# Regrouping the PSUM banks of a transformer-block kernel: score buffers, dense sums and the transposed maxima

## The chip, the cores and the metric

The kernel runs on one core of a Trainium2 chip. The metric is the device time of one launch in microseconds (us). It is the median of three runs for the kernel before, and a profiled execution of its own stands beside it.

A core has five engines that run side by side, each through its own list of instructions in order: TensorE (PE) multiplies matrices, VectorE (DVE) and ScalarE (ACT) work element by element and can read PSUM, GpSimd (POOL) works on SBUF, and SyncE (SP) issues DMAs. TensorE writes its results to PSUM, which has eight banks of 128 partitions x 512 fp32 values. A bank can be written again only when the engines that read it are done.

## The reference

One transformer block for 16 batches of 512 tokens and 512 channels, in fp32: attention with 32 heads of 16 channels, rotated by position, causal, and then a gated feed-forward layer of 1408 inner channels with weights of -1, 0 and 1. Cut to what matters:

```
x  = inputs                                     # 16 x 512 x 512
n  = layernorm(x)
q, k, v = n @ Wq.T + bq, n @ Wk.T + bk, n @ Wv.T + bv
q, k = rope(q), rope(k)                         # by head, two rotations
p  = softmax(causal(q @ k.T / 4))               # 32 heads, 512 x 512
x  = x + layernorm((p @ v) @ Wo.T + bo)
n  = layernorm(x)
g, u = (n @ gate_w.T) * gate_s, (n @ up_w.T) * up_s
x  = x + layernorm((silu(g) * u) @ down_w.T * down_s)
```

## The kernel before

**Periods, groups, steps.** `front` prepares batch 0 and part of batch 1. Then `batches` runs one period for each batch `b`. In a period the attention of batch `b` is computed in 8 groups of 4 heads, each in `STEPS = 6` steps (`one_step(work, n, i)`, group `n`, step `i`). The dense products of the neighbouring batches are laid between the steps: `run_list` takes a list of single matmuls, each with a cost, and lets a share of it follow the scores of each step. For `b = 0` the list is `first_list`, which holds little: the rest of v, then q and k of batch 1, the transposes of batch 2's normalised input, and `fold_bias`. It is spread over 56 steps, ten of which come ahead of the first group (`n = -2` and `-1`), so that a step carries about one dense matmul. From `b = 1` on the list holds a whole batch's products, and a step carries four to ten dense matmul records. This document calls the steps of `b = 0` the first period.

**A step.** `scores(n, m, i)` emits two kinds of scores, each for two heads, with their matmuls interleaved head by head:

- `st`, the scores of group `n` with keys on the partitions, minus the row maxima (`mx`), which the last of each three matmuls adds. ScalarE makes the softmax weights of them (`weights`: an exponential `pt<-st`), and GpSimd then zeroes what lies beyond the diagonal. `i // 2` is the third of the keys' triangle: 512 columns, 128 + 384 columns, 256 columns. `i % 2` is the pair of heads.
- `s`, the scores of a coming group `m` with queries on the partitions. VectorE takes their negative row maxima (`maxima`, instructions `s<-s,mask` with a readout `nm`).

At step 2 `turn_maxima` transposes the maxima of group `n + 1` on TensorE (`pm`), ScalarE and VectorE split them into two parts (`nmh`, `nml`), and DMAs put these into `mx`. Then the step's share of dense matmuls comes. At step 3 and at step 0 of the next group `values` multiplies weights and values (`av`), 8 records at step 3 and 24 at step 0, and at the end ScalarE copies the sum out (`ot`).

**Dense sums.** `product` takes a bank with `psum` at its first matmul and calls a `tail` after its last. For q and k (`qk_block`, products `pq` and `pk`) the tail is two ScalarE instructions `ys` and one VectorE instruction `ya`, both reading the bank. Some items later follow `ya<-ya,ys` (VectorE), `yh` (ScalarE) and `yl` (GpSimd). For the transposes of a normalised block (`turn`, `px`, four transposes into one bank) the tail is a ScalarE copy, in the first period `ht<-px`. For `pv` it is a copy to `v`; for `fold_bias` (`po`) a VectorE addition.

**The eight banks.** `ps_s` holds two tiles `s` of one bank; `ps_t` one tile `st` of two banks; `ps_av` one bank `av`; `ps_d` three banks in turn, for all that `psum` hands out: the dense sums and `pm`. Ahead of the first group (`n < 0`) the steps with odd `i` put their `s` scores into the `st` tile.

The names in the profile are those of the tiles; line 49 is a helper that records every operation, so the names, not the lines, tell what an instruction is.

Of the kernel before, what the change touches and what calls it, by code (L numbers as in the profile page):

```python
# [10 lines left out]
FP = mybir.dt.float32  # L11
FR = mybir.dt.float32r
AF = mybir.ActivationFunctionType
# [5 lines left out]
P = 128  # L19
T = 512  # L20
# [18 lines left out]
class InOrder:  # L39


    def __init__(self, tc, engine):
        self.tc, self.engine = tc, engine
# [10 lines left out]
class Block:  # L54
# [15 lines left out]
    def __init__(self, tc, ctx, a):  # L70
        self.tc, self.a = tc, a
        nc = self.nc = tc.nc
        self.pe = InOrder(tc, nc.tensor)
        self.dve = InOrder(tc, nc.vector)
        self.act = InOrder(tc, nc.scalar)
        self.pool = InOrder(tc, nc.gpsimd)
        self.sp = InOrder(tc, nc.sync)
        self.B = a["x"].shape[0]
        self.F = a["wd"].shape[0]
        self.NF = self.F // P  # L80
        pool = lambda name, **k: ctx.enter_context(tc.tile_pool(name=name, **k))
        self.const = pool("const", bufs=1)
        self.work = pool("work", bufs=2)
        self.small = pool("small", bufs=5)
        self.dram = pool("dram", bufs=1, space=bass.MemoryType.DRAM)
        self.ps_s = pool("ps_s", bufs=2, space=bass.MemoryType.PSUM)
        self.ps_t = pool("ps_t", bufs=1, space=bass.MemoryType.PSUM)
        self.ps_av = pool("ps_av", bufs=1, space=bass.MemoryType.PSUM)
        self.ps_d = pool("ps_d", bufs=3, space=bass.MemoryType.PSUM)
        self.todo = defaultdict(list)  # L90
        self.step = 0
        self.exact = False

        self.spare = [(self.B - 2, 2), (self.B - 2, 3), (self.B - 1, 3)]
        for name in "xts xns xnts x1s x2ts ks qs mxs nms pts avs ots ocs rcs wts hts wfs yas xrs pieces".split():
            setattr(self, name, {})
        self.constants()
# [3 lines left out]
        return (pool or self.work).tile(shape, dtype, tag=tag, name=tag, **kw)  # L101

    def psum(self, name):
        return self.ps_d.tile([P, 512], FP, tag="d", name=name)

    def later(self, steps, f, *args):
        self.todo[self.step + steps].append((f, args))
# [454 lines left out]
    def scores(self, n, m, i):  # L562

        third, pair = divmod(i, 2)
        ps = pm = None
        todo = []
        if 0 <= n < self.B * NG:
            ps = self.ps_t.tile([P, 2, T], FP, tag="st", name="st")
            q, ks, mx = self.qs[n], self.ks[n], self.mxs[n]
            for j in range(2):  # L570
                h = 32 * (2 * pair + j)
                r, r2 = slice(h, h + 32), slice(h, h + 2)
                todo.append([])
                for kb, at, w in ST_SETS[third]:
                    out, x = ps[:, j, at : at + w], q[r, T - w : T]
                    todo[-1] += [
                        (out, ks[0][r, ts(kb, P)], x, True, False),
                        (out, ks[1][r, ts(kb, P)], x, False, False),
                        (out, self.one[r2, :], mx[r2, T - w : T], False, True),
                    ]  # L580
        if 0 <= m < self.B * NG:
            if n < 0 and i % 2:
                both = self.ps_t.tile([P, 2, T], FP, tag="st", name="st")
                pm = [both[:, j, :] for j in range(2)]
            else:
                pm = [self.ps_s.tile([P, T], FP, tag="s", name="s") for _ in range(2)]
            q, ks = self.qs[m], self.ks[m]
            for j in range(2):
                h = 32 * (2 * (1 - pair) + j)
                r = slice(h, h + 32)  # L590
                todo.append([])
                for qb, at, w in S_SETS[third]:
                    out, x = pm[j][:, at : at + w], q[r, ts(qb, P)]
                    todo[-1] += [(out, x, ks[0][r, 0:w], True, False), (out, x, ks[1][r, 0:w], False, True)]

        for k in range(max((len(t) for t in todo), default=0)):
            for t in todo:
                if k < len(t):
                    out, l, r, first, last = t[k]
                    self.pe.matmul(out, l, r, start=first, stop=last)  # L600
        if ps is not None:
            self.weights(n, third, pair, ps)
        if pm is not None:
            for j in range(2):
                self.maxima(m, third, 2 * (1 - pair) + j, pm[j])
# [9 lines left out]
            )  # L615

    def turn_maxima(self, m):
        p = self.psum("pm")
        self.pe.transpose(p[0:16, 0:P], self.nms.pop(m).rearrange("p j b -> p (j b)"), self.ident)
        hi, lo = [self.tile([16, P], i, bufs=1, dtype=FR) for i in ("nmh", "nml")]  # L620
        self.act.copy(hi, p[0:16, 0:P])
        self.dve.tensor_tensor(lo, p[0:16, 0:P], hi, ALU.subtract)
        mx = self.mxs[m] = self.tile([P, T], "mx", bufs=2, dtype=FR)

        def put():
            for i, t in enumerate((hi, lo)):
                self.sp.dma_start(out=mx[i:P:32, :].bitcast(FP), in_=t.bitcast(FP))

        self.later(1, put)

    def weights(self, n, third, pair, ps):
        w = sum(w for _, _, w in ST_SETS[third])
        if third < 2 or pair == 0:
            pt = self.tile([P, 2, T], "pt", bufs=4)
            self.pts[n, third, pair] = pt
        if third == 2:
            if pair:
                pt = self.pts[n, 2, 1] = self.pts[n, 2, 0]
            pt = pt[:, pair, :].rearrange("p (j t) -> p j t", j=2)
        self.act.activation(pt[:, :, :w], ps[:, :, :w], AF.Exp, scale=0.25)  # L640
        if third == 1:
            d = pt[:, :, 0 : 2 * P]
            pat = [[0, 2], [0, 2], [1, P]]
        else:
            d = pt[:, :, 0:P]
            pat = [[0, 2], [1, P]]
        self.pool.affine_select(out=d, in_=d, compare_op=ALU.is_ge, fill=0.0, base=0, pattern=pat, channel_multiplier=-1)
# [303 lines left out]
    def batches(self):  # L951
        B = self.B
        work = self.run_list(self.first_list(), 56)
        self.load_group(0)
        for n, i0 in ((-2, 2), (-1, 0)):
            for i in range(i0, STEPS):
                self.one_step(work, n, i)
        for b in range(B):
            if b:
                if b < B - 1:  # L960
                    L = self.dense(b)
                    L += self.gate_ups(b - 1, b + 2 if b + 2 < B else None, b + 2 == B)
                    if b < B - 2:
                        L += self.downs(b - 1, b + 2)
                else:
                    down = [self.downs(b - 2, None, tbs, True, True) for tbs in ((0, 1), (2, 3))]
                    L = down[0] + self.dense(b, down[1]) + self.gate_ups(b - 1, None, True)
                work = self.run_list(L, NG * STEPS)
            for g in range(NG):
                for i in range(STEPS):  # L970
                    self.one_step(work, b * NG + g, i)
        L = [(0, lambda half=half: self.load_w(B - 1, "o", half)) for half in range(2)]
        work = self.run_list(L + self.downs(B - 2, None, (0, 1), True, True), STEPS + 2)
        for i in range(STEPS + 2):
            self.one_step(work, B * NG + i // STEPS, i % STEPS)
        for _, f in self.laid(self.last_list()):
            f()
# [61 lines left out]
```

## Time and profile before

| | |
|---|---|
| median of 3 runs | 3222.02 us (3218.17 to 3222.62) |
| profiled execution | 3215.86 us, of which the span 3214.0 us |
| busy share of the span | PE 96%, DVE 59%, ACT 48%, POOL 43% |
| 108 to 260 us, the first period's groups | PE busy 128.34 of 152.00 us, mean clock 0.85 |
| 260 to 3054 us, the later periods | PE busy 2752.18 of 2794.00 us, mean clock 1.00 |
| exponential `pt<-st`, 128x1024 and 128x512 | 1.024 us and 0.596 us |

How to read it: the page divides the span into 40 slices of 80 us and gives each engine's busy share in tenths; `PEclk` is the clock granted to TensorE in tenths of full speed. "Waits" list who waited for whom: total us, how often, the longest. In the timeline a line is start, duration, engine, operation, out<-in with the shape, and in brackets the idle time just before it and what ended it. `PEld` is the load of a matmul's stationary operand, which can run beside a matmul. An fp32 matmul of the dense products appears as two records, so that "x2" there is one matmul. Durations come from one execution, so a sum made of them is measured against 3215.86 us.

### The profile page before, as it was taken

How to read it: one execution, taken by the hardware profiler on the slowest of the kernel's cores; microseconds unless marked ns; L12 is line 12 of the kernel's file. 1: busy time of each engine (PE TensorE's matmuls, PEld its weight loads, DVE VectorE, ACT ScalarE, POOL GpSimd, SP SyncE). 2: the span in 40 equal slices, each digit the busy share in tenths (PEclk: the TensorE clock that was granted, in tenths of full speed). 3: DMA queues.
4: the chain of work that ended last, by engine and by line, in shares of the span. 5: the costliest groups of instructions: out<-in, count | busy, mean ns of one | idle time of the engine just before them, and what ended most of it. 6: DMA issues, size and time to landing. Idle time of an engine off the chain costs nothing.

```text
span 3214.0 us, 59287 instructions
## 1 busy us (share of the span) xinstructions
PE 3097.9 (96%) x21258; PEld 1743.3 (54%) x21258; DVE 1888.0 (59%) x5911; ACT 1542.7 (48%) x2243; POOL 1383.9 (43%) x1933
## 2 busy tenths in 40 slices
PE   6889999999999999999999999999999999999988
PEld 2334555646556464655646455464655646455556
DVE  5465656556565665656566565665656566565633
ACT  5354545454554544545454554544455454453432
POOL 4143445443544534345443544534345453443343
PEclk9899999999999999999999999999999999999999
DMA  6454534445353443525345352543535345343422
GB/s 251 166 166 152 189 101 163 139 149 172 108 190 106 160 164 123 195 93 177 127 152 173 127 185 96 168 147 123 195 101 183 122 147 172 123 156 105 131 97 71
DMA packets 227441, 471.41 MB, mean 147 GB/s; under 512 B 40976, under 2 KB 45072, under 8 KB 226704
## 3 DMA queue, kind: packets, MB, share of 16 engines
q1 hardware_dynamic: 226704, 466.47, 43.1%
q8 instruction: 170, 2.79, 0.4%
q10 hardware_dynamic: 432, 1.05, 0.1%
q14 instruction: 135, 1.11, 0.1%
HBM read 345.79 MB, written 125.30 MB: 147 GB/s over the span
## 4 chain that ended last, share of the span: by engine, by line
PE 83%; DVE 2%; DMA 2%; ACT 2%; POOL 1%; issue 1%; SPq 0%; ACTq 0%; DVEq 0%; POOLq 0%
PE st L49 16%; PE pu L49 11%; PE pg L49 10%; PE av L49 9%; PE pd L49 9%; PE po L49 7%; PE pq L49 6%; PE pv L49 5%; PE pk L49 5%; PE s L49 3%; DMA kl<-kd 2%; PE px L49 1%; ACT pt L49 1%; DVE s L49 1%; PE pm L49 1%
## 5 line engine op out<-in xcount | busy, mean ns | idle before, releaser
L49 DVE CUSTOM_DVE_ANT_0 s<-s,mask 128x512 f32<-128x512 f32 (+1 forms) x2034 | 974.9, 510 | 713.8 <-PE s L49 530.8
L49 ACT ACTIVATE pt<-st 128x1024 f32<-128x1024 f32 (+1 forms) x768 | 677.0, 882 | 755.9 <-PE st L49 746.9
L49 POOL TENSOR_SCALAR_AFFINE_SELECT pt<-pt 128x256 f32<-128x256 f32 (+1 forms) x768 | 393.8, 513 | 1202.3 <-ACT pt L49 1200.0
L49 PEld LDWEIGHTS st<-q,kh 32*128 32x128 f32 x2048 | 191.3, 183 | 463.3 <-issue 225.6
L49 PE MATMUL st<-q,kh 32*128 32x512 f32 (+3 forms) x2048 | 411.2, 398 | 22.3 <-ACT pt L49 20.9
L49 PE MATMUL s<-kh,q 32*128 32x512 f32 (+1 forms) x2034 | 411.6, 399 | 17.2 <-DVE nm L49 8.8
L49 PE MATMUL s<-kl,q 32*128 32x512 f32 (+1 forms) x2034 | 340.7, 321 | 11.2 <-DMA kl<-kd 11.2
L49 PE MATMUL av<-pt,v 128*32 128x512 f32 (+3 forms) x4096 | 336.0, 447 | 0.0
L49 PE MATMUL st<-q,kl 32*128 32x512 f32 (+3 forms) x2048 | 333.5, 322 | 0.0
L49 PE MATMUL st<-mx,one 2*128 2x512 f32 (+3 forms) x2048 | 333.0, 321 | 0.0
L49 POOL TENSOR_TENSOR hl<-ht,hh 128x512 fp32r<-128x512 f32 (+1 forms) x192 | 229.6, 1196 | 184.3 <-ACT hh L49 176.7
L49 PE MATMUL pd<-wd,hl 128*128 128x512 f32 x704 | 288.9, 410 | 9.2 <-POOL hl L49 9.2
L49 PE MATMUL pd<-wd,hh 128*128 128x512 f32 x704 | 290.9, 413 | 2.2 <-ACT hh L49 2.2
L49 DVE DVE_READ_ACCUMULATOR2_ANT nm<- 128x1 f32 x2048 | 288.8, 141 | 0.0
L49 PE MATMUL pg<-xntf,wf 128*128 128x512 f32 x704 | 287.4, 408 | 1.5 <-ACT xntf L49 1.5
L49 PE MATMUL pu<-xntfl,wf 128*128 128x512 f32 x704 | 284.3, 404 | 0.0
L49 PE MATMUL pu<-xntf,wf 128*128 128x512 f32 x704 | 283.9, 403 | 0.0
L49 PE MATMUL pg<-xntfl,wf 128*128 128x512 f32 x704 | 281.5, 400 | 0.6 <-DVE xntfl L49 0.6
L49 PE MATMUL po<-w,oc 128*128 128x512 f32 x512 | 244.6, 610 | 3.7 <-DMA w<-in_wo 3.7
L49 PE MATMUL pq<-xnta,w 128*128 128x512 f32 x480 | 237.6, 626 | 6.9 <-ACT xntf L49 6.3
L49 PE MATMUL pk<-xnta,w 128*128 128x512 f32 x480 | 238.3, 615 | 4.3 <-DVE ya L49 3.7
L49 POOL TENSOR_TENSOR yl<-ya,yh 128x512 fp32r<-128x512 f32 x128 | 163.3, 1276 | 169.4 <-ACT yh L49 169.4
(118 smaller groups left out, 5021.8 us busy)
## 6 DMA issues: line engine op xcount, KB each, us to landing
wf<-wgs SPq DMA_DIRECT2D x176, 512.0 KB
q<-qd SPq DMA_DIRECT2D x128, 256.0 KB
kh<-kd SPq DMA_DIRECT2D x128, 256.0 KB
kl<-kd SPq DMA_DIRECT2D x128, 256.0 KB
od<-ot SPq DMA_DIRECT2D x128, 256.0 KB
w<-in_wo SPq DMA_DIRECT2D x34, 512.0 KB
xr<-in_x SPq DMA_DIRECT2D x66, 256.0 KB
w<-in_wq SPq DMA_DIRECT2D x32, 512.0 KB
```

The costliest lines, as they stand in the source:

```text
L49: return self.tc.keep_in_program_order(f(*args, **kwargs))
```

## The change

In the first period (and in the ten steps ahead of it) only one of the three banks of `ps_d` serves the dense sums. The other two become a second place for `st`, used in the steps with odd `i`, while even steps use `ps_t` as before; ahead of the first group they take the odd steps' `s` scores. As two one-bank tiles take the place of one two-bank tile there, the exponential of an odd step is two instructions, one for each head, instead of one. From the second period on the three banks serve the dense sums in turn again and every step uses `ps_t`. In all periods `pm` is put into the bank of `av` and no longer takes a turn among the three.

```diff
-        self.ps_d = pool("ps_d", bufs=3, space=bass.MemoryType.PSUM)
+        self.ps_d = pool("ps_d", bufs=1, space=bass.MemoryType.PSUM)
+        self.banks, self.bank = 3, 0
...
     def psum(self, name):
-        return self.ps_d.tile([P, 512], FP, tag="d", name=name)
+        self.bank = (self.bank + 1) % self.banks
+        return self.ps_d.tile([P, 512], FP, tag=f"d{self.bank}", name=name)
+
+    def two_banks(self, other, name):
+        if other and self.banks == 1:
+            return [self.ps_d.tile([P, T], FP, tag=f"d{1 + j}", name=name) for j in range(2)]
+        return self.ps_t.tile([P, 2, T], FP, tag="st", name=name)
...
     def scores(self, n, m, i):
...
-            ps = self.ps_t.tile([P, 2, T], FP, tag="st", name="st")
+            ps = self.two_banks(i % 2, "st")
...
             if n < 0 and i % 2:
-                both = self.ps_t.tile([P, 2, T], FP, tag="st", name="st")
-                pm = [both[:, j, :] for j in range(2)]
+                pm = self.two_banks(True, "s")
...
     def turn_maxima(self, m):
-        p = self.psum("pm")
+        p = self.ps_av.tile([P, T], FP, tag="av", name="pm")
...
     def weights(self, n, third, pair, ps):
...
-        self.act.activation(pt[:, :, :w], ps[:, :, :w], AF.Exp, scale=0.25)
+        if isinstance(ps, list):
+            for j in range(2):
+                self.act.activation(pt[:, j, :w], ps[j][:, :w], AF.Exp, scale=0.25)
+        else:
+            self.act.activation(pt[:, :, :w], ps[:, :, :w], AF.Exp, scale=0.25)
...
     def batches(self):
...
+        self.banks = 1
         for n, i0 in ((-2, 2), (-1, 0)):
...
             if b:
+                self.banks = 3
```

More of the change, by code (lines that the diff above doesn't have):

```diff
@@ L574, in scores @@
                 for kb, at, w in ST_SETS[third]:
-                    out, x = ps[:, j, at : at + w], q[r, T - w : T]
+                    out, x = (ps[j] if isinstance(ps, list) else ps[:, j])[:, at : at + w], q[r, T - w : T]
                     todo[-1] += [
```

## The prediction

> **What bounds the kernel now.** I read the page first: TensorE is busy for 3097.9 of 3214.0 us, and its slices say where it is not.
>
> ```profile
> PE   6889999999999999999999999999999999999988
> PEclk9899999999999999999999999999999999999999
> ```
>
> Only the first three slices and the tail are below 9. Then busy time by stage: from 260 to 3054 us PE has 2752.18 of 2794.00 us at clock 1.00, so dense matmuls bound it there. In the first period's 48 steps, 108 to 260 us, it has 128.34 of 152.00 us at a clock of 0.85. That is the room: 23.7 us idle and 0.15 x 152 = 23 us of withheld clock. Third, the waits of 120 to 260 us:
>
> ```profile
> PEld st L49 <- ACT pt L49: 32.9, 32, 2.3
> PE st L49 <- ACT pt L49: 13.0, 14, 2.0
> PE s L49 <- DVE nm L49: 4.9, 13, 0.7
> ```
>
> A weight load can wait beside a running matmul, so the price of one score buffer `st` looks like the second line, 13.0 us in 14 waits. The timeline tells whether it is. Such a wait:
>
> ```profile
> 180.48 0.60 ACT L49 ACTIVATE pt<-st 128x512 f32<-128x512 f32 x1 [0.74 <-PE st L49]
> ...
> 180.66 0.47 DVE L49 CUSTOM_DVE_ANT_0 s<-s,mask 128x256 f32<-128x256 f32 x1
> ...
> 181.13 0.38 PE L49 MATMUL st<-q,kh 32*128 32x256 f32 x2 [0.75 <-ACT pt L49]
> ```
>
> PE resumes when the exponential ends. But the same step's `s` matmuls, next in PE's queue, need the maxima of the last step to be read, and that VectorE instruction ends at 180.66 + 0.47 = 181.13 too. The other pair of banks is free no earlier.
>
> Fourth, the end of a dense sum, the place where one bank must do for three:
>
> ```profile
> 181.69 1.13 PE L49 MATMUL pk<-xnta,w 128*128 128x512 f32 x2
> ...
> 182.65 0.27 PE L49 MATMUL px<-ident,xn 128*128 128x128 f32 x1
> ...
> 182.91 1.38 ACT L49 ACTIVATE ys<-pk,cols 64x512 f32<-64x512 f32 x2
> ...
> 184.38 0.75 DVE L49 SCALAR_TENSOR_TENSOR ya<-pk,cols,turn 128x512 f32<-128x512 f32 x1 [1.79 <-PE px L49]
> ```
>
> `pk` ends at 182.8, and its bank is read by `ys` and then by `ya`, to 185.13. The transposes `px` start at 182.65 only because they have another bank.
>
> [...] 2 us of gaps are enough for it here:
>
> ```profile
> 196.00:200.00 4.00, 2.10 (x18) 0.97 (x17) 1.86 (x6) 3.26 (x6) 2.72 (x3) 1.00 0.43 145
> 200.00:204.00 4.00, 3.88 (x12) 1.43 (x12) 3.04 (x11) 1.42 (x2) 2.65 (x4) 0.58 0.72 247
> ```
>
> (PE, PEld, DVE, ACT and POOL busy, then the clock.) [...] in all eight q and k sums of the period `ya` starts 0.08 to 0.10 us after `ys` ends. [...] an exponential ready early waits behind `yh` and `ys` there.
>
> **The change, part by part.** Apart from the exponentials, every engine keeps its instructions in their order; SP's and POOL's queues, and so all DMAs and selects, pass nothing new.
>
> *Exponentials of odd steps, split in two.* 24 of 48 steps. A 128x1024 one takes 1.024 us, a 128x512 one 0.596: 2 x 0.596 - 1.024 = 0.17. 128x256 isn't in the trace; on the line through the two it takes 0.38, again 0.17 more (bounds: 0, and 0.596 if halving saves nothing). 24 x 0.17 = 4.1 us of ScalarE, hidden by its 83 idle us in the period (68.97 of 152 busy), except where `ys` is queued behind: there `ys`, `ya`, the maxima behind `ya` and the next `s` come 0.17 late. That is so at two of the q sums (near 123 and 154 us): +0.3 us.
>
> *The wait of `st` goes.* I went through all 14. In each the second head's `s` matmul is held by VectorE to within 0.2 us of where it is now: by the maxima alone where a step has no dense matmul (143.5, 165.0, 181.2), by maxima queued behind a `ya` otherwise (142.20, 174.01, 200.95, 219.95, 236.9). 0 to 0.15 us each; I take -0.5 us of the 13.0. What is late next is the `s` bank.
>
> *One bank for dense sums.* A bank is free at `ya`'s end: 0.1 + 1.38 + 0.09 + 0.75 + 0.1 = 2.4 us after the last matmul, and later when ScalarE has `yh` or an exponential first. PE waits in order: behind the dense matmul stand the next scores and `av`, and for these ScalarE's exponentials and VectorE's maxima. Taken turn by turn from the times of before:
> - `pq` to `pq` near 137.7: the bank is free at 140.4 (`ya` ends at 140.31), a stall of 2.7 us. Before, PE reached the next scores early and was held by VectorE to 142.2; these scores now end near 143.1 for 142.7. +0.4.
> - `pq` to `pq` near 156.1 (free 157.3) and `pq` to `pk` near 170.8 (free 171.7): the next `s` is held to 158.99 and 174.01 anyway. 0. Near 127.2 the bank has long been free.
> - `pk` to `px` near 182.7: free at 185.35. One transpose 0.2, scores 0.9, three transposes 0.5, `av` 1.45, scores 0.9: to 189.3, where they ended at 187.17. VectorE would have been done. +2.1.
> - `pk` to `px` near 197.4: free at 200.15, after 0.6 of transposes scores from 200.75; before, `s` was held to 200.95. 0.
> - `pk` to `px` near 216.8: free at 219.15; the following two scores end near 221.6 for 220.62. +0.95.
> - `pk` to `px` near 233.3: free at 236.1, scores at 236.6; before held to 236.9. 0. But the fourth transpose now stands straight ahead of `po`, which must wait for the copy out of `px` (exponential to 238.25, copy 0.58): 237.55 to 238.85. +1.2.
> - `px` to `pk`, three times: a step of scores or `av` lies between. 0.
>
> Sum 4.65. Unhidden the stalls would be 2.7 + 1.2 + 0.9 + 2.65 + 2.7 + 2.35 + 2.8 + 1.3 = 16.6 us, the upper bound; the lower is 0.
>
> *Clock.* The gap at 182.7 is new: 180 to 188 us runs at 1.00 now. With 2.65 us of idle like that ahead of 200 I expect one more half-clock spell. The spell at 240 cost: `po` 2.08 for 1.12, `av` 2.79 for 1.50, scores some 0.5: 2.8 us. Bounds: one spell less, -2.8, and two more, +5.6. I take +2.8.
>
> *Maxima in the bank of the values, in all 128 groups.* New waits: `pm` for the copy `ot` of the group before, made two steps earlier (131.8 to 132.4 for a `pm` at 134.86); `av` for `nmh` and `nml` (`nml` ends at 176.84, `av` starts at 178.76; the smallest slack that I saw is 1.9 us, and a later step is longer). 0. Gone is the wait of `pm` for a ring bank, 6.1 us in 13 later periods, always at one place:
>
> ```profile
> 341.17 0.28 PE L49 MATMUL pm<-ident,nm 128*16 128x128 f32 x1 [0.44 <-DVE ya L49]
> ...
> 343.59 0.32 PE L49 MATMUL s<-kh,q 32*128 32x128 f32 x1 [0.17 <-DVE nm L49]
> ```
>
> One step on, PE waits for maxima that are queued behind that same `ya` and end at 343.5 whatever PE does. The second gap grows by what the first loses: 0 (bounds -6.1 and 0).
>
> Sum: 0.3 - 0.5 + 4.65 + 2.8 + 0 = +7.25 us. The profiled execution took 3215.86 us about its span of 3214.0; I expect 3223.1 there. The median of the runs is 6.2 us above it: 3222.02 + 7.25 = 3229.3 us.
>
> **Rivals.** *The `st` wait is the limit.* All 13.0 us go, and with them two spells (2 x 2.8): -13.0 - 5.6 + 4.65 + 0.3 = -13.6, 3208.4 us, faster. For it: the profile puts the waits on `pt`, and the worst (1.90, 2.03) stand just ahead of spells. Against: the VectorE ends above. It decides from the point where waits and spells saved pass 4.95 + 6.4 = 11.4 us.
>
> *The later `pm` wait is worth its 6.1 us.* +7.25 - 6.1 = +1.2, 3223.2 us, no change. Against: 343.59.
>
> *The turns cost little.* Without the new spell, and with VectorE covering more: +0 to +5, about 3225, no change.
>
> *Little is hidden.* 16.6 + 5.6 - 0.5 = +21.7, 3243.7 us.
>
> **The numbers.** 0.2%, 6.4 us, is about what a measurement of this kernel can tell from no change. Chances: forecast 0.45, little hidden 0.08, both slower: 0.53. Turns cheap 0.22, `pm` 0.10: same 0.32. `st` the limit, by itself or by luck with the clock: faster 0.15. The range runs from -8 (half-way into the fast case) to +18 (most of the way to the unhidden sum): 3214 to 3240. The forecast's own range is 3225.5 to 3234.
>
> **What would show it.** Right: the wait of `st` for `pt` near zero in 120 to 260 us, `s` for `nm` well up, new waits of `px`, `pq` and `po` for `ya` or a copy, some 12 to 17 us in about eight places; a low clock near 188; 260 to 3054 us as long as before, `pm` without a wait, and the following `s` waiting 0.6 for 0.17. Wrong: the stretch from 108 us to the first `pv` of the second period shorter than now, or the clock in it above 0.85.

## The result and the profile after

The changed kernel takes 3232.76 us (median of 7 runs, 3227.08 to 3238.59); the kernel before took 3217.09 us in the 7 runs shown with them. The ratio is 1.0051, with a 95% interval from 1.0035 to 1.0067: 11 to 22 us slower, 16 us at the middle. The forecast was 3229.3 us, 7 us slower than before, in a range that holds the result. The sign was right and the size too small. That the time itself came within 3.5 us of the forecast is luck: the kernel before read 3217.09 us in these seven runs and 3222.02 in the three from which the forecast started. The profiled execution took 3232.76 us too, 16.9 us above that of before, so the two traces stand for their kernels.

The page of the changed kernel, busy slices and clock:

```profile
PE   6889999999999999999999999999999999999988
PEclk9888999999999999999999999999999999999999
```

The third and fourth slices (160 to 320 us) have lost a tenth of clock; nothing else on the two rows has moved. To see how much of the 16.9 us that is, I took the stretch from the first `st` of the first group to the first `pv` of the second period, in both traces. It holds the same TensorE work (978 and 979 records). Busy time by engine, then clock, first before and then after:

```profile
108.42:259.56 151.14, 127.59 (x978) 55.15 (x978) 83.16 (x297) 68.62 (x96) 51.55 (x75) 0.85 0.50 168
```

```profile
108.50:272.50 164.00, 135.12 (x979) 57.82 (x978) 82.80 (x297) 70.74 (x120) 51.31 (x75) 0.79 0.47 156
```

The first period is 12.9 us longer. Idle time grew from 151.14 - 127.59 = 23.55 to 164.00 - 135.12 = 28.88 us, so by 5.3; 0.9 of these are one wait for a key transfer (`s` for `kh`, 4.8 us for 3.9). The other 7.5 us are matmuls that took longer, at a mean clock of 0.79 for 0.85. ScalarE's 24 further instructions are the split exponentials: 70.74 - 68.62 = 2.1 us, for the 4.1 that I had estimated. The last 4 us arise later in small pieces (below).

The waits of PE in that stretch after, as engine, tile, releaser: total us, times, longest:

```profile
PE px L49 <- DVE ya L49: 10.2, 4, 2.8
PE s L49 <- DVE nm L49: 8.4, 18, 1.2
PE s L49 <- DMA kh<-kd: 4.8, 1, 4.8
PE pq L49 <- DVE ya L49: 3.6, 2, 2.6
PE po L49 <- ACT ht L49: 0.8, 1, 0.8
```

The 13.0 us of `st` for `pt` are gone. In their place stand 14.6 us of `px`, `pq` and `po` for the one dense bank, and `s` for `nm` went from 4.9 to 8.4. So 13.0 us of waits were taken away, and idle time rose.

The turn that the prediction expected near 188 us, in the timeline after (PE; then the end of the sum on ScalarE and VectorE):

```profile
184.86 1.13 PE L49 MATMUL pk<-xnta,w 128*128 128x512 f32 x2
188.43 0.48 PE L49 MATMUL px<-ident,xn 128*128 128x128 f32 x1 [2.44 <-DVE ya L49]
...
190.41 0.90 PE L49 MATMUL px<-ident,xn 128*128 128x128 f32 x3
```

```profile
186.15 1.38 ACT L49 ACTIVATE ys<-pk,cols 64x512 f32<-64x512 f32 x2
187.62 0.75 DVE L49 SCALAR_TENSOR_TENSOR ya<-pk,cols,turn 128x512 f32<-128x512 f32 x1 [1.85 <-ACT ys L49]
```

`pk` ends at 185.99, `ys` and `ya` read its bank until 188.37, and `px` starts 0.06 us later. Before, the first `px` ran just ahead of `ys` and the other three beside it. ScalarE's order shows there too: scores complete at 181.75 us got their exponential at 182.29, behind `yh`, and those complete at 183.90 at 184.31, 0.02 us after the end of `ys`. And the transposes behind the stall are slow: 0.48 us for one and 0.90 for three, where the kernel before took 0.27 for one. The same place by windows:

```profile
184.00:188.00 4.00, 1.94 (x10) 0.78 (x10) 2.15 (x8) 2.80 (x6) 2.88 (x4) 0.86 0.94 266
188.00:192.00 4.00, 3.57 (x26) 2.11 (x30) 2.27 (x6) 1.42 (x2) 1.20 (x2) 0.50 0.91 345
192.00:196.00 4.00, 4.00 (x31) 1.37 (x23) 1.76 (x7) 1.76 (x4) 0.91 (x3) 0.79 0.16 56
```

PE is busy for 1.94 of 4 us, and about 7 us at half clock follow (clocks of 0.86, 0.50 and 0.79 in three windows of 4 us are 1.1 + 4 + 1.7 us of it). This document calls such a stretch a spell. The stalls before 208.07, 228.42 and 247.21 us do the same (0.50, 0.50 and 0.54 in the 4 us from 208, 228 and 248 us), and the one before 143.96 us is followed by 12 us at 0.50.

### The profile page after: what moved, and what is told of

Its sections match the earlier page's. It is cut to its first block, busy times and chain, and to the rows that moved or that the text cites. A ratio compares the mean times of both kernels' runs of the same rounds, so it can differ in the third digit from the quotient of the medians.

```text
span 3231.0 us, 59381 instructions
## 1 busy us (share of the span) xinstructions
PE 3106.9 (96%) x21258; PEld 1747.7 (54%) x21258; DVE 1889.0 (58%) x5911; ACT 1545.7 (48%) x2267; POOL 1386.5 (43%) x1933
## 4 chain that ended last, share of the span: by engine, by line
PE 82%; DVE 3%; DMA 3%; ACT 2%; POOL 1%; issue 1%; SPq 0%; ACTq 0%; DVEq 0%; POOLq 0%
PE st L49 15%; PE pu L49 11%; PE pg L49 10%; PE pd L49 9%; PE av L49 9%; PE po L49 6%; PE pq L49 6%; PE pv L49 5%; PE pk L49 5%; PE s L49 3%; DMA kl<-kd 2%; PE px L49 1%; DVE s L49 1%; PE pm L49 1%; ACT pt L49 1%
## 5 line engine op out<-in xcount | busy, mean ns | idle before, releaser
L49 DVE CUSTOM_DVE_ANT_0 s<-s,mask 128x128 f32<-128x128 f32 (+3 forms) x2048 | 981.2, 510 | 726.7 <-PE s L49 544.6
L49 ACT ACTIVATE pt<-st 128x1024 f32<-128x1024 f32 (+2 forms) x792 | 678.9, 860 | 767.1 <-PE st L49 760.5
L49 PE MATMUL s<-kh,q 32*128 32x128 f32 (+3 forms) x2048 | 417.2, 399 | 30.9 <-DVE nm L49 20.8
L49 PE MATMUL s<-kl,q 32*128 32x128 f32 (+3 forms) x2048 | 345.0, 322 | 12.0 <-DMA kl<-kd 11.9
```

What stands on the lines that cost most here:

```text
L49: return self.tc.keep_in_program_order(f(*args, **kwargs))
```

## The experiments

**Theory.** The wait of the scores was not the limit; one dense bank puts stalls of 2 to 3 us ahead of five dense matmuls; the stalls lengthen the period by some 5 us, and by more through the half clock that follows them. **Rivals.** The second place for `st` brings its 13 us but something else eats them; `pm` in the bank of the values costs in the later periods; the difference comes from elsewhere.

All results in one table, in us but for the ratios and the clock. Ratios are against the kernel before, run on the same chip; the change and the experiments ran on several chips. Length, busy, idle and clock are those of the first period's stretch as above, from one profiled execution each. The last two columns are means over all runs: the record of a run has its span and its mean granted clock, span x (1 - clock) is called withheld, and the remainder of the span is called the rest. Each is given less that of before on the same chip; for the change, less the mean of the four such sets of before (50.7 and 3166.0 us). The withheld column is good to some 3 to 5 us (95%), the rest to 1 to 3 us.

| | ratio [95% interval] | length | PE busy | idle | clock | withheld, runs | rest, runs |
|---|---|---|---|---|---|---|---|
| before | 1 | 151.1 | 127.6 | 23.6 | 0.85 | 0 | 0 |
| the change | 1.0051 [1.0035, 1.0067] | 164.0 | 135.1 | 28.9 | 0.79 | +6.5 | +8.2 |
| e1, one place for `st` | 1.0040 [1.0024, 1.0056] | 156.3 | 126.4 | 29.8 | 0.84 | +5.6 | +7.9 |
| e2, only `pm` moved | 1.0025 [1.0014, 1.0036] | 147.2 | 126.3 | 20.9 | 0.87 | +4.7 | +2.6 |
| e3, `pm` back later | 1.0170 [1.0139, 1.0200] | 155.4 | 127.9 | 27.5 | 0.85 | +8.8 | +44.9 |
| e4, change + copy | 1.0012 [1.0001, 1.0022] | 145.3 | 125.2 | 20.1 | 0.87 | 0.0 | +3.4 |
| e5, `pm` moved early | 1.0011 [1.0002, 1.0019] | 155.0 | 133.4 | 21.6 | 0.81 | +1.2 | +1.4 |
| e6, change + fillers | 1.0001 [0.9992, 1.0010] | 142.8 | 123.0 | 19.8 | 0.95 | -10.3 | +10.9 |
| e7, before + copy | 0.9988 [0.9975, 1.0000] | 144.1 | 120.4 | 23.8 | 0.89 | -4.4 | -0.7 |
| e8, third bank for `s` | 1.0002 [0.9987, 1.0017] | 139.0 | 117.5 | 21.4 | 0.89 | -3.4 | +2.8 |
| e9, e6, one place for `st` | 0.9996 [0.9985, 1.0006] | 149.3 | 127.3 | 22.0 | 0.90 | -13.1 | +10.0 |
| e10, before + fillers | 0.9987 [0.9978, 0.9997] | 140.8 | 126.5 | 14.4 | 0.94 | -11.9 | +7.3 |
| e11, e7 + fillers | 0.9986 [0.9973, 0.9998] | 133.2 | 117.0 | 16.2 | 0.99 | -11.1 | +6.1 |
| e12, e10 + `pm` moved | 0.9982 [0.9965, 0.9999] | 148.7 | 134.8 | 14.0 | 0.87 | -10.9 | +5.4 |

One warning for reading it. In this period e2 and e5 are the same program, and their idle times agree (20.9 and 21.6), but their busy times do not: 126.3 and 133.4 us for the same 978 or 979 records. How often the clock falls differs from one execution to the next: over the runs of one kernel the withheld part of the span scatters by 3.5 to 7 us (standard deviation). So two traces can differ by some 15 us of busy time through chance, and such a difference needs the ratios or the last columns. The idle column can be compared trace by trace, but for one wait in it: `s` for the key transfer `kh` takes 1.7 to 4.8 us in these traces (3.9 before, 4.8 in the change, 1.7 in e10 to e12).

**e1: one dense bank, and one place for the scores.** The edit to the changed kernel:

```diff
-            ps = self.two_banks(i % 2, "st")
+            ps = self.two_banks(False, "st")
```

> The change with its second place for the weights' scores left out: in the first period one bank serves the dense sums and every step uses the one tile st (exponentials whole again); the maxima stay in the bank of the values. Theory (the single dense bank costs the time, and a second st place is worth next to nothing, as VectorE holds s at the same moment): about what the whole change has, +12 to +17 us over before. Rival (the second st place does earn most of the 13.0 us of waits for pt, and the dense bank costs more than was thought): +25 us or more.

Measured: 1.0040, 13 us slower than before, as the theory had it. Its waits in 108 to 262 us:

```profile
PE px L49 <- DVE ya L49: 10.1, 4, 2.7
PE st L49 <- ACT pt L49: 5.9, 7, 1.2
PE pq L49 <- DVE ya L49: 3.5, 2, 2.6
```

One place for `st` costs nothing that the ratios tell apart from two. Of the 13.0 us of its waits only 5.9 are left although that buffer is as it was: the dense stalls stand ahead of them and take their place. Apart from the one dense bank, e1 differs from before by the place of `pm`, by the counter that hands out the banks (see e3) and by the place of the `s` scores of the odd early steps. It has nearly the whole loss.

**e4: the dense bank freed early.** The changed kernel, with each q and k sum of the first period copied to SBUF by ScalarE, so that `ys` and `ya` read the copy:

```diff
+            if self.first:
+                pc = self.tile([P, T], "sg", bufs=2)
+                self.act.copy(pc, p)
+                p = pc
```

> The change, and in the first period the end of each q and k sum copies the dense bank to SBUF first (one ScalarE copy of 128x512, 0.58 us), and ys and ya read the copy. So the bank is free some 0.8 us after the last matmul instead of 2.4, plus what ScalarE has queued, and ya no longer stands behind ys. Theory (the time is the stalls of px, pq and po for the bank, 14.6 us in the change's trace, and the clock that they cost): the stalls fall to 4 to 7 us, the clock of the first period comes back to 0.85 or more, and the kernel is 8 to 14 us faster than the change, -2 to +6 us against before. Rival (VectorE's maxima hold the steps whatever the dense bank does): within 4 us of the change.

Measured: 1.0012, some 12 us better than the change, as the theory had it. The waits of `px`, `pq` and `po` for the bank fall from 14.6 to 5.2 us (`sg` is the copy):

```profile
PE px L49 <- ACT sg L49: 3.5, 4, 1.2
PE pq L49 <- ACT sg L49: 0.9, 1, 0.9
PE po L49 <- ACT ht L49: 0.8, 1, 0.8
```

Idle time falls by 8.8. The instructions that the change added are not the cause, since e4 has these too; the time that the bank is held is. But not all of the 12 us belong to it: the same copy takes 4 us off the kernel before (e7), where no dense sum waits for its bank in this period. The difference of the two gains is 0.0027 with about +-0.0023, some 9 us.

**e6: the stalls filled with matmuls that nobody reads.** Two dense 128x512 matmuls ahead of each set of transposes `px` and of the third query sum, written to the place for `st` that the step does not use:

```diff
+    def warm(self):
+        t = self.two_banks((self.i + 1) % 2, "warm")
+        out = t[0] if isinstance(t, list) else t[:, 0, :]
+        x = self.xnts["a", 1]
+        for k in range(2):
+            self.pe.matmul(out, x[:, k, 0:P], x[:, k, :], start=True, stop=True)
```

> The change, with two dense matmuls whose result nobody reads put ahead of the four sets of px and of the third pq sum of the first period, where PE stood 2.3 to 2.8 us for the single dense bank. They write to the place of st that is free then, take 2.1 us at full clock and so fit into the stall; all that the change computes stays. Theory (the stalls cost twice, by themselves and by the half clock that follows; in the change's trace 5.3 us of the first period's +12.9 were idle and 7.6 longer matmuls): the clock of 108 to 260 us rises from 0.80 to 0.85 or more and the kernel is 4 to 8 us faster than the change. Rival (the spells come from elsewhere): no faster than the change, or 1 to 3 us slower.

Measured: 1.0001, for 1.0051 without them. I had expected a part of the loss back; all of it came back. The window of its first period, and the groups of the fillers (records, busy us, mean ns):

```profile
106.70:249.54 142.84, 123.02 (x999) 54.33 (x998) 82.47 (x297) 70.40 (x120) 51.30 (x75) 0.95 0.51 174
```

```profile
L49 PE MATMUL warm<-xnta 128*128 128x512 f32 x20 | 9.7, 608 | 0.0
```

The ten fillers take 9.7 us of PE (1.88 for the pair at 209.65 us, at a clock of 1.00), and idle time falls by 28.9 - 19.8 = 9.1: for the bank PE waits as long as ever, only busily. Without the clock nothing would be won. But the other matmuls take 123.0 - 9.7 = 113.3 us for 135.1. By the two traces that is 22 us; by the ratios it is 16, and 0.6 for what the fillers take over the idle time that they remove. The runs agree: from the change to e6 the withheld part falls by 16.8 us and the rest rises by 2.7, so what came back is clock. It is more than the change had lost that way (6.5 us by the table), since the kernel before has such spells too: fillers of its own take 11.9 us of withheld clock from it (e10).

**e9: e6 with one place for the scores**, to see what the second place is worth when the clock is steady.

> The kernel of e6 (unread dense matmuls ahead of the four transposes' turns and of the third query sum) with the weights' scores held in one place, as before: one dense bank, the other place for the scores stays empty but for the unread products. The waits of a scores for the exponentials come back (e1 had 5.9 us of them). Theory (with the clock kept up, what is left of the change is its small waits): ratio to e6 within 0.998 to 1.002, so 0.998 to 1.002 of the kernel before, granted clock 0.90 or more in 108 to 260 us. Rival (the second place is worth what it was meant to bring, and the change's gain was only covered by the clock): 6 us or more above e6, that is a ratio to the kernel before of 1.002 or more, with 6 to 13 us of waits of a scores in the first period.

Measured: 0.9996 for e6's 1.0001. The second place is worth -0.0005 with an interval of about +-0.0015: 3 us won at most, and probably nothing. Yet e9 shows the waits that it removes:

```profile
PE st L49 <- ACT pt L49: 6.8, 9, 1.2
...
PE s L49 <- DVE nm L49: 3.1, 10, 0.5
```

In e6 the first row is absent, and the second reads 9.3 us in 20 waits. The 6.8 us moved to the other row, 6.2 of them. This is the prediction's reading of the `st` waits, shown with the fillers in both kernels; the rival that the second place brings its 13 us falls. The clock of 0.89 in 108 to 260 us came out just below what I had asked for.

**e2 and e5: only `pm` moved**, in all periods and in the first alone.

```diff
-        p = self.psum("pm")
+        p = self.ps_av.tile([P, T], FP, tag="av", name="pm")
```

> The kernel before with one part of the change alone: the transposed maxima go to the bank of the values, in all periods. Theory (the 0.47 us that pm no longer waits in 13 periods is taken back one step later by s waiting for maxima): within 1 us of before; pm without waits for ya and the following s waits 0.6 us instead of 0.17. Rival (those waits are worth their sum): 6 us faster. Second rival (the new waits of av for the split maxima bite, and explain the 3 us or so by which the change is slower outside the first period): 3 to 6 us slower.

> The kernel before, with the transposed maxima in the bank of the values in the first period only (three dense banks in turn throughout, st as before); from the second period on they take their turn among the three banks of the ring, so this run differs from the one with the maxima moved in all periods only in the later periods. Theory A (moving them costs in the later periods, by a mechanism not yet named): within 2 us of before, and 5 us or more faster than that run. Theory B (the later periods of that run were slower by chance, from how its DMA waits and half-clock spells fell): the two runs within 3 us of one another.

Measured: 1.0025 and 1.0011, both slower than before. e2 lies outside what my theory allowed, and `av` never waits for the split maxima in it, so the mechanism of the second rival is not there either. e5 is 0.0014 below e2 with about +-0.0014, some 4.5 us, and fits neither of its two theories. The traces show the mechanism as predicted (see the point on `pm` below), with nothing lost at that place. The two intervals overlap, and e5, with `pm` back among the three banks from the second period on, is 3.5 us slower for no reason that its trace shows but slower matmuls. By the last columns e2 loses 4.7 us of clock and 2.6 us besides. These two runs did not settle it.

**e3: the changed kernel with `pm` among the three banks from the second period on.**

```diff
-        p = self.ps_av.tile([P, T], FP, tag="av", name="pm")
+        p = self.ps_av.tile([P, T], FP, tag="av", name="pm") if self.banks == 1 else self.psum("pm")
```

> The change with the maxima in the bank of the values in the first period only; from the second period on they take their turn among the three dense banks again, as before. Theory (only the first period counts): as slow as the whole change, +12 to +17 us over before. Rival (pm in the values' bank costs in later periods): +10 us or less. Rival (it gains there): +19 us or more.

Measured: 1.0170, missed by all. Its waits from 280 to 3054 us:

```profile
PE pk L49 <- DVE ya L49: 27.7, 14, 2.1
PE s L49 <- DMA kl<-kd: 14.9, 13, 2.1
...
PE pm L49 <- DVE ya L49: 6.8, 13, 0.9
```

The changed kernel hands out its banks by a counter, `d0`, `d1`, `d2`. With `pm` in the count a k sum meets a bank whose `ya` is not done, in each later period; these waits are 27.7 of the 39 us by which the trace of e3 is longer than that of the change. The kernel before, with `pm` in the same turn, has 1.1 us of that wait: its pool of three buffers does not seem to keep to a strict order. So e3 is no test of `pm` alone. It shows that the counter is safe only because `pm` was taken out of it.

**e12: `pm` moved, with the first period's clock kept up.** e10 below with the edit of e2 (and a second product named `pm`, made once in the whole launch, moved too), to try the same question again.

> The kernel of e10 (the kernel before with unread dense matmuls in its first period) with the transposed maxima pm in the bank of the values, in all periods. Nothing is left out of the computation. Theory (the place of pm costs and brings nothing, since the scores wait for the maxima one step later; e2's 1.0025 came from where the spells at half clock fell): ratio to the kernel before within 0.0010 of e10's 0.9987, that is 0.9977 to 0.9997. Rival (pm in the bank of the values costs some 8 us in the later periods): 0.9997 to 1.0025, 4 to 12 us above e10, with the difference in 280 to 3054 us, as waits of s for nm of 15 us or more or a lower clock there.

Measured: 0.9982, for 0.9987 without the move; the theory's range holds it. The difference is -0.0005 with about +-0.0020. So with the fillers the move shows no cost: the rival's 8 us are excluded, 4 us are not. The loss of e2, clear of zero over 22 runs, stays unexplained, and whether `pm` costs a few us in the later periods is open. Between the 16th and the 128th `pm` the traces with `pm` there take longer (+) or shorter (-) than before by +3.6 (the change), +11.1, +12.2, +13.3, +8.3, +13.4, -3.3 and +5.6 us (e1, e2, e4, e6, e8, e9, e12), those with `pm` among the three +5.5, 0.0, +2.4 and +1.8 (e5, e7, e10, e11). The means, 8.0 and 2.4, point to a small cost; the spread, on several chips, is as large as the difference.

**e7 and e8: other uses of the room.** e7 is the kernel before with the copy of e4. e8 gives the freed bank to `s` (three banks in turn), keeps two for dense sums and one place for `st`.

> The kernel before, and in the first period the end of each q and k sum copies the bank to SBUF first (0.58 us of ScalarE), and ys and ya read the copy, so that ya need not stand behind ys. Three dense banks and one st as before. Theory (VectorE's maxima queued behind the late ya hold s, and they come up to 1.4 us earlier in eight places, of which st's own wait for pt, now 0.58 later, hides a part): 0 to 6 us faster than before. Rival (the first period's steps are held by ScalarE's queue as much): 2 to 5 us slower, as eight copies stand ahead of exponentials.

> The change turned about: in the first period two banks serve the dense sums in turn, st has one place, and the third dense bank joins the two of s, so that the maxima's scores go round three banks. Maxima in the values' bank as in the change. Theory (both st and s hold a step to within 0.2 us, so that relief of one alone is worth little; two dense banks are enough): the first period within 3 us of before, no px or pq wait for ya above 0.5 us, and with what the moved maxima seem to cost later +3 to +9 us over before. Rival (s was the tighter of the two and a third bank frees it): the first period 6 us or more shorter than before.

Measured: 0.9988 and 1.0002. e7 is as its theory had it; that `ya` need not stand behind `ys` when both read the copy, in e4 too, was my estimate and is not shown here. e8 fits neither side: the first period of its trace is 12 us shorter, though only 2.2 us of this are idle time, where the theory had it within 3 us; and the ratio shows nothing, where the theory had 3 to 9 us more. In e8 `s` for `nm` falls to 1.0 us in 3 waits and no dense sum waits for its bank; now `st` for `pt` has 13.4. Against before, the third bank takes away `nm`'s wait and leaves the other as it was, the change the other way round: in this step two waits end at nearly the same time (within 0.2 us in the trace of before), and removing either shows little.

**e10 and e11: fillers for the kernels without the change.** In the first period alone, by what dense work the step had: two 128x512 ahead of step 2, one after transposes alone, one 128x256 where there was none.

```diff
+        if 0 <= n < NG:
+            if n == 0 and i == 1:
+                self.warm(2)
+            elif self.did == "px":
+                self.warm(1)
+            elif not self.did:
+                self.warm(1, T // 2)
```

> The kernel before with unread dense matmuls in the first period alone: two 128x512 ahead of the second step, where the scores wait for a key transfer; one 128x512 after each step whose dense work is transposes alone; one 128x256 in each step without dense work. Nothing is left out of the computation. Theory (the clock falls after short idle stretches, and a spell at half clock costs more than the matmuls that prevent it): clock 0.92 or more in 108 to 260 us for 0.85, waits of a scores for the exponentials shorter by the fillers' own time, 5 to 12 us faster, ratio 0.996 to 0.9985. Rival (each filler delays the step's scores by what it saves): 0 to 6 us slower, ratio 1.000 to 1.002, whatever the clock does.

> The fillers of e10 on the kernel of e7 (the kernel before, with each query and key sum of the first period copied out of its bank by ScalarE ahead of its normalization). Nothing is left out of the computation. Theory: e7's gain (0.9988) and e10's add up, 8 to 15 us faster than before, ratio 0.995 to 0.9975. Rival (fillers are worth nothing, or both remove the same idle time): no faster than e7, ratio 0.998 to 1.000.

Measured: 0.9987 [0.9978, 0.9997] and 0.9986 [0.9973, 0.9998], 4 us faster than before each. e10 has its clock (0.94) and a first period 10.3 us shorter, and is faster as the theory said, but by 4 us, just short of its 5 to 12; its fillers cost 11.9 us of PE. e11 is within the rival's range: copy and fillers do not add up by the ratios, although its trace shows the period 17.9 us shorter. That profiled execution is the fastest of its 14 (3197.74 us, median 3210.91), so its trace flatters it. e7, e10, e11 and e12 are the versions that beat both kernels, by 0.12 to 0.18%; their intervals overlap and end at 0.9997 to 1.0000.

## Why the prediction was right, and where it was too small

**The `st` wait (-0.5): right.** Of the 13.0 us, 3 at most were worth having by e9 and 4 at most by e1, and probably none.

**One dense bank (+4.65): right.** The stalls were to be 16.6 us unhidden in eight places and came to 14.6 in seven: 2.61 for 2.7, 0.96 for 1.2, 2.44 for 2.65, 2.70 for 2.7, 2.31 for 2.35, 2.78 for 2.8, 0.83 for 1.3, and none for 0.9 at the `pk` near 170.8. Most of it lies beside VectorE's work: with the split exponentials and the `st` term I had 4.45 us of added idle time, and 5.3 were measured, 4.4 without the key transfer. In e1 it is 29.8 - 23.6 = 6.2. e2 and e5, which keep three banks, have less idle time than before, so this part belongs to the bank and not to `pm`.

**The clock (+2.8): the term that was mis-sized.** I counted one new spell, at the one gap that looked new, and let the other stalls fall into places that had a slow clock already. In the trace the matmuls of the first period took 7.5 us longer, which one execution can show by chance. Over the runs the clock withheld 6.5 us more than before, with about +-4. Summed over windows of 4 us with a clock below 0.85, from 108 to 276 us, before withholds 22.2 us and the change 33.8. The same places set side by side (the change is 4 us late at 150 and 12 at 250), the spell near 188 came as forecast (+2.8 of withheld clock). Behind the stalls at 144, 228 and 247 us, where before had spells too, they are longer: 140 to 156 for 140 to 152, 228 to 236 for 220 to 224, 248 to 260 for 236 to 244 us, +6.1 in all. These are stalls that I had costed at 0 to 0.95 us since VectorE hid them. Two more spells (128 to 136 and 220 to 224, +5.0) stand behind no stall of the dense bank, and one of before (160 to 164, -1.5) is gone; for these I have no cause, and they are of the size that e2 and e5 differ by. So I read it thus: VectorE's work hid these stalls as a delay, but not from the clock. PE stood for 2.61, 2.31 and 2.78 us at the three places all the same, and the stretches behind them withheld the 6.1 us more. e6 shows that filling these stalls brings the clock back; how much of the 6.5 us is theirs alone is not shown.

The size of these gaps is in the trace: the 4 us around each of the five, 2.3 to 2.8 us long, were busy for 1.1 to 2.1 us only, and the next window of 4 us ran at 0.50 to 0.54. The place where the prediction called 2 us of gaps enough for a lower clock is of this kind: in the kernel before PE stood for 1.90 us ahead of 199.97, and 200 to 204 us ran at 0.58. Both kernels have such spells, the change more of them (33.8 us withheld for 22.2), and e6 shows their price in it: 1.0051 to 1.0001.

**`pm` in the bank of the values (0): right at its place, open elsewhere.** After the change, at the place where before had 0.44 and 0.17:

```profile
353.89 0.28 PE L49 MATMUL pm<-ident,nm 128*16 128x128 f32 x1
356.84 0.32 PE L49 MATMUL s<-kh,q 32*128 32x128 f32 x1 [0.58 <-DVE nm L49]
```

The wait of `pm` is gone and `s` waits 0.58 us, as forecast at 0.6. VectorE's own row explains it: its `ya` was at 340.36 before and is at 353.61 now, 13.25 later, and the `ya<-ya,ys` behind the maxima was at 343.60 and is at 356.85, 13.25 later again. What PE gained ahead of it made VectorE no earlier. The later periods as a whole, waits of PE from 280 to 3060 us, before and then after:

```profile
PE s L49 <- DMA kl<-kd: 11.2, 13, 2.5
...
PE pm L49 <- DVE ya L49: 6.1, 13, 0.5
PE s L49 <- DVE nm L49: 4.0, 17, 0.5
```

```profile
PE s L49 <- DMA kl<-kd: 11.9, 13, 1.4
PE s L49 <- DVE nm L49: 11.3, 21, 0.6
```

6.1 + 4.0 = 10.1 us became 11.3, so the rival that gave 3223.2 us falls. I had said that 260 to 3054 us would be as long as before; 3.6 us were added there between the 10th and the last `pm`. I can't attribute them, and other kernels drift by up to 13 us (e12 above). Nor do the runs divide the 16 us between the bank and `pm`. With the copy the change is still 0.0024 above its counterpart (e4 over e7), with fillers 0.0014 (e6 over e10), and `pm` alone has 0.0025 (e2), each with some +-0.0011 to 0.0016; only e12 speaks against a cost of `pm`. My 0 for it is not shown. Besides the clock the runs of the change are 8.2 us longer, by the last column, for the 4.45 of the other terms; 4.4 of them stand in the first period, and what is left came where I had put nothing.

**The rivals' chances.** The fast case (all `st` waits and two spells) is excluded by e9. "Little is hidden" (3243.7 us) had the total nearer than the forecast had by the ratio (+16 against +21.7 and +7.25), but in part for another reason than its own: of 14.6 us of stalls 5.3 became idle time in the first period, for its 16.6, while its clock term (+5.6) was about right.

## What to carry to other kernels

Before you shorten a buffer's rotation to serve a wait, ask what ends next behind that wait: here VectorE's maxima ended within 0.2 us of the exponential, and of 13 us of waits 3 at most were worth having. Count every stall of TensorE twice, once as delay (which other engines may hide: here 14.6 us of stalls became 5.3 us of idle time) and once as a gap with a lower clock behind it (here 0.50 to 0.54 in the next window of 4 us, for five gaps of 2.3 to 2.8 us). Where a stage has such gaps, either shorten the time a bank is held (a copy out took 12 us off the changed kernel, and 4 off the kernel before) or fill the gaps with matmuls that nobody reads (16 us off the changed kernel).

## What was not expected of the hardware

- Ten unread matmuls, 9.7 us of TensorE, made the changed kernel 16 us faster; 11.9 us of them made the kernel before 4 us faster.
- In the change, gaps of 2.3 to 2.8 us in a thinly filled step were followed by 7 to 14 us at half clock, and the same instructions (e2 and e5) differed by 7 us of TensorE time between two executions, 126.3 us at a mean clock of 0.87 and 133.4 at 0.81.
- Where two waits end within 0.2 us of each other, their times in the profile did not tell what removing one is worth. Freeing one bank at a time moved 13.0 us from `pt` to `ya` and `nm` (the change), and 4 us from `nm` to nothing with `pt` at 13.4 (e8), at no gain in time that the ratios show.
